# Order of ScalarE's exponentials in a two-state selective scan, and the pace at which two stages are interleaved

## Chip, cores and metric

The kernel runs on one core of one Trainium2 chip. A core has five engines with instruction streams of their own: TensorE (PE in the profile, its weight loads PEld), VectorE (DVE), ScalarE (ACT), GpSimd (POOL) and SyncE (SP), which issues the DMAs. The metric is the device time of one execution in microseconds (us), the median of several runs.

## The reference

Four layers run over an image batch of shape 4 x 64 x 64 x 96. Layers 0 and 1 are selective scans over the image in four directions; layers 2 and 3 are attention without softmax and a quantised feed-forward block. The scan layers take nearly all the time. Each computes, after a group norm, an input projection, a 3x3 depthwise convolution and a SiLU:

```python
xs = jnp.concatenate([xs2, jnp.flip(xs2, axis=-1)], axis=1)        # 4 directions
x_dbl = jnp.einsum('bkdl,kcd->bkcl', xs, x_proj_weight)
dts, Bmat, Cmat = jnp.split(x_dbl, [DT_RANK, DT_RANK + D_STATE], axis=2)
dts = jnp.einsum('bkrl,kdr->bkdl', dts, dt_projs_weight)
delta = jax.nn.softplus(dts + dt_projs_bias[None, :, :, None])
A = -jnp.exp(A_logs).reshape(K, D_INNER, D_STATE)

def step(h, inp):                        # over the 4096 pixels
    u_l, dl, b_l, c_l = inp
    dA = jnp.exp(dl[..., None] * A)
    h = dA * h + (dl * u_l)[..., None] * b_l[:, :, None, :]
    y = jnp.einsum('bkdn,bkn->bkd', h, c_l)
    return (h, y)
```

There are 192 channels and 16 states per channel. The four directions' y are added, normalised over channels, gated with silu(z) and projected back to 96 channels, and the layer's input is added.

## The kernel before, in words

**Units.** A scan layer works on its four images in two pairs, so there are four units (two layers by two pairs). The 2 x 192 channels of a pair fill three tiles of 128 partitions: j = 0 and 1 are 128 channels of one image each ("own"), j = 2 holds 64 channels of each ("shared"). A unit has 48 steps: 4 directions k, 4 chunks ci of T = 1024 pixels, 3 tiles j (`PairScan.steps`).

**Groups.** A step's 16 states are worked two at a time, in eight groups of NG = 2 (`groups` in `PairScan.scan`). For each state the chip needs `exp(delta * A)` and the product `(delta * u) * B`, then one tensor_tensor_scan on VectorE that makes `h`; GpSimd multiplies `h` by C in place, and TensorE adds the states up in PSUM (`yp`) by transposing `h` into it. The letters in `OWN` and `SHARED` (line 45) say which engine makes a state's product:

- V: TensorE selects the row of B into a PSUM tile `bp`, and VectorE multiplies it by `du`.
- A: ScalarE makes the product in transposed form (`x`, `outer`: 8 instructions, 16 for j = 2), and TensorE transposes it into `bp`.
- G: GpSimd multiplies `du` by a row of B that a DMA has spread over the partitions (`dbu`). Then `bp` is free, and ScalarE writes this state's exponential into it.

For V and A the exponential goes into an SBUF tile `da` (four buffers). `bp` has two buffers, one for each state of a group. In letters, a step of an own tile is VA VA VA AG VA VA VA VA, and a step of the shared tile VG VA VA VG VA VG VA VV.

**Order.** Inside the scan all compute engines keep program order (`InOrder`), so the order of the calls in the loop of lines 680 to 730 is the order on each engine. For group g it is:

1. `start_bp` for both states of g (TensorE's products; for a G state ScalarE's exponential into `bp`).
2. `sum_of(g - 3)`: TensorE adds up an older group.
3. `start_ahead(g + 1)`: the next group's `da` and `x` on ScalarE. `start_cb` and `start_dbu` start its DMA and GpSimd's products.
4. VectorE: the V product of g, then its two scans. A group AG has no V product, and its two scans follow each other directly.
5. Pieces of the following steps' preparation (`drive`: `project`, `discretise`), at fixed groups. At state 4 of each step this is softplus (`delta`), followed by `finish_sum`, ScalarE's copy of the finished sum `yp` to `ysum`. Softplus needs another activation table, so there is a table load before it and one before the next exponential.
6. GpSimd: `last` (the carry to the next chunk) and h times C.

**Between the scans.** `between_scans` prepares the next unit (`scan_inputs`: norm, input projection, convolution, first pieces of the scan; a generator with 20 yields) and finishes the unit before (`scan_outputs`: norm over channels, gate, output projection; 16 yields, one for each 256 pixels). Three of these stages are joint: both generators have work, and a loop takes one output and then some inputs in turn. Instructions here do not keep program order strictly; a planner places them at compile time, with the order of the calls as priority. `scan_outputs` takes its tiles from a pool with two buffers, three for the last unit, which runs together with the token layers.

Of the kernel before, what the change touches and what calls it, by code (L numbers as in the profile page):

```python
# [40 lines left out]
NG = 2  # L41
# [100 lines left out]
def between_scans(tc, cst, ident, half, pn, u, before, scan, after):  # L142


    with ExitStack() as stage:
        ins = scan_inputs(tc, stage, cst, ident, half, pn, u, scan, *after)
        if before is not None:
            pp = stage.enter_context(tc.tile_pool(name="c_ps", bufs=2, space=PSUM))
            outs = scan_outputs(tc, stage, cst, ident, half, pn, *before, pp)
            for _ in outs:  # L150
                for _ in range(2):
                    next(ins, None)
        for _ in ins:
            pass
# [117 lines left out]
def scan_outputs(tc, stage, cst, ident, half, pn, layer, pr, pp, turned="pt", summed="po"):  # L272

    nc = tc.nc
    par, zg, x_src, x_dst, y = layer.par, layer.zg[pr], layer.x_src, layer.x_dst, layer.y[pr]
    p2 = stage.enter_context(tc.tile_pool(name="c2", bufs=3 if layer.last and pr else 2))
    if not layer.last:
        norms = [GroupNorm(p2, pn, f"gn{2 * pr + i}", NT // 2) for i in range(2)]
    wo = p2.tile([128, 3, C], F32, name="wo", bufs=1)
# [2 lines left out]
    for g in range(NT // 2):  # L282
# [46 lines left out]
        bufs = 1 if summed == "po" else None  # L329
# [31 lines left out]
def load_weights(nc, pk, w, k):  # L361

    wx = pk.tile([128, 3, NC], F32, name="wx")
    nc.sync.dma_start(out=wx, in_=w["wx"][k])
    wdt = pk.tile([NC, 3, 128], F32, name="wdt")
    nc.sync.dma_start(out=wdt, in_=w["wdt"][k])
    return wx, wdt


class PairScan:  # L370
# [116 lines left out]
    def scan(self, stage, nc):  # L487
        tc, ident, steps, projected, made = self.tc, self.ident, self.steps, self.projected, self.made
# [3 lines left out]
        p2 = stage.enter_context(tc.tile_pool(name="b_2", bufs=2))  # L492
# [4 lines left out]
        def begin_project(k, ci):  # L497
            return self.project(nc, nc.gpsimd, odd if ci % 2 else self.pq, pm, "m1", k, ci)

        def begin_discretise(at):  # L500
            return self.discretise(nc, nc.gpsimd, odd if at % 2 else self.pq, pm, ("m0", "m1"), at)
# [13 lines left out]
        groups = [(at, n) for at in range(len(steps)) for n in range(0, NS, NG)]  # L515
        of = (0, 128, 64)

        def maker(g, i):
            at, n0 = groups[g]
            return (SHARED if steps[at][2] == 2 else OWN)[n0 + i]  # L520

        def exp_of(out, g, i):

            at, n0 = groups[g]
            k, _, j = steps[at]
            col = k * NS + n0 + i
            nc.scalar.activation(out, made[at][0], AF.Exp, scale=amat[:, j // 2, col : col + 1])

        def start_ahead(g):

            at, n0 = groups[g]
            das, xs = {}, {}
            for i in range(NG):
                if maker(g, i) == "A":
                    xs[i] = outer(g, i)
                if maker(g, i) != "G":
                    das[i] = p2.tile([128, T], F32, name="da", bufs=4)
                    exp_of(das[i], g, i)
            return das, xs

        def outer(g, i):

            at, n0 = groups[g]
            j = steps[at][2]
            dut, bt = made[at][2], projected[at // 3][4]
            x = p2.tile([128, T // 128, 128], F32, name="x")
            for t in range(T // 128):
                for im, cols in ((0, slice(0, D1)), (1, slice(D1, 128))) if j == 2 else ((j, slice(0, 128)),):
                    col = NS * im + n0 + i
                    nc.scalar.mul(x[:, t, cols], dut[:, t, cols], bt[:, t, col : col + 1])  # L550
            return x
# [5 lines left out]
            spread(cb, projected[at // 3][2], steps[at][2], n0)  # L557
            return cb

        bbs = {}  # L560

        def start_bb(g):

            at, n0 = groups[g]
            for i in range(NG):
                if maker(g, i) == "G":
                    bbs[g, i] = p2.tile([128, 1, T], F32, name="bb", bufs=1)
                    spread(bbs[g, i], projected[at // 3][2], steps[at][2], 2 * NS + n0 + i)
# [9 lines left out]
        def start_bp(g, i, xs):  # L578


            at, n0 = groups[g]
            _, _, j = steps[at]
            bp = pm.tile([128, T], F32, name="bp", bufs=2)
            if maker(g, i) == "G":
                exp_of(bp, g, i)
            elif maker(g, i) == "A":
                for t in range(T // 128):
                    nc.tensor.transpose(bp[:, 128 * t : 128 * t + 128], xs[i][:, t], ident)
            else:
                for hf in range(2):  # L590
                    cols = slice(512 * hf, 512 * hf + 512)
                    nc.tensor.matmul(
                        bp[:, cols],
                        sel[:, n0 + i, of[j] : of[j] + 128],
                        projected[at // 3][1][:, cols],
                        start=True,
                        stop=True,
                    )
            return bp
# [31 lines left out]
        def start_skip(at):  # L631

            k, _, j = steps[at]
            if k == 0:
                skips[at] = p2.tile([128, T], F32, name="skip", bufs=1)
                nc.scalar.mul(
                    skips[at].rearrange("p (a b) -> p a b", b=HW), projected[at // 3][0][j], dsum[:, j // 2]
                )
# [15 lines left out]
        def load_kept(at):  # L654

            if steps[at][0]:
                kept[at] = p2.tile([128, T // 128, 128], F32, name="kept", bufs=1)
                for tile_, there in places(at, kept[at]):
                    nc.sync.dma_start(out=tile_, in_=there)
# [12 lines left out]
        def sum_of(g):  # L672
            for i in range(NG):
                add_up(g, i, hs[g])
            del hs[g]

        def begun(pieces):
            return [next(pieces), pieces]

        for g, (at, n0) in enumerate(groups):  # L680
            k, ci, j = steps[at]
            rev, first, final = k >= 2, ci == 0, ci == L // T - 1
            if n0 == 0:
                if first and j == 0:
                    last = [pk.tile([128, NS], F32, name=f"last{i}", tag=f"last{i}") for i in range(3)]
                    if k + 1 < K:
                        weights[k + 1] = load_weights(nc, pk, w, k + 1)
                if j == 0:
                    projecting = begun(begin_project(*steps[at + 3][:2])) if at + 3 < len(steps) else []
                discretising = begun(begin_discretise(at + 1)) if at + 1 < len(steps) else []  # L690
            if n0 == 8 and at + 1 < len(steps):
                load_kept(at + 1)
            (da, xs), cb, dbu = ahead, cb_next, dbu_next
            if g + 2 < len(groups):
                start_bb(g + 2)

            bps = [start_bp(g, i, xs) for i in range(NG)]
            if g >= LAG:
                sum_of(g - LAG)
            if n0 == 0:  # L700
                start_skip(at)
            if n0 == NS - NG:
                drive(discretising, n0)
                drive(projecting, (j, n0))
            if g + 1 < len(groups):
                ahead, cb_next, dbu_next = start_ahead(g + 1), start_cb(g + 1), start_dbu(g + 1)

            hs[g] = h = p2.tile([128, NG, T], F32, name="h", bufs=LAG + 1)
            du = made[at][1]
            for i in range(NG):  # L710
                if maker(g, i) == "V":
                    nc.vector.tensor_tensor(bps[i], du, bps[i], ALU.mult)
            way = slice(None, None, -1) if rev else slice(None)
            for i in range(NG):
                nc.vector.tensor_tensor_scan(
                    h[:, i, way],
                    (da[i] if i in da else bps[i])[:, way],
                    (bps[i] if i in da else dbu[i])[:, way],
                    0.0 if first else last[j][:, n0 + i : n0 + i + 1],
                    ALU.mult,  # L720
                    ALU.add,
                )
            drive(discretising, n0)
            if n0 == NG * (LAG - 1) and at > 0:
                finish_sum(at - 1)
            drive(projecting, (j, n0))
            if not final:
                nc.gpsimd.tensor_copy(last[j][:, n0 : n0 + NG], h[:, :, 0] if rev else h[:, :, T - 1])
            for i in range(NG):
                nc.gpsimd.tensor_tensor(h[:, i], h[:, i], cb[:, i], ALU.mult)  # L730
# [363 lines left out]
```

## Time and profile before

The median of three runs is 10643.59 us (10634.33 to 10654.25). The profiled execution took 10644.94 us, its span is 10643.2 us, and all times below are of it.

| | PE | DVE | ACT | POOL |
|---|---|---|---|---|
| busy us in the span | 8055.8 | 9608.1 | 8760.2 | 9008.7 |
| share | 76% | 90% | 82% | 85% |
| busy in 5200 to 7500 (a scan stage) | 1753.31 | 2173.41 | 1988.56 | 2153.91 |
| busy in 7500 to 7720 (a joint stage) | 179.58 | 136.35 | 123.86 | 28.13 |

From first to last, the span holds a first preparation (to about 156 us), scan 0, a joint stage from about 2461 to 2680, scan 1, a joint stage to about 5199, scan 2, a joint stage to about 7715, scan 3 to about 10014, and the token layers with the last outputs.

A row of groups gives line, engine, operation, the tiles written and read, shapes and number, then busy time and mean length of one, then the idle time of the engine ahead of them and what ended it. Nearly all scan instructions carry line 71, that of the helper that keeps their order, so they are told apart by their tiles. Durations of one instruction that matter: a scan 2.3 us, a V product 1.2 us, an exponential 1.1 us, the eight x together 2.4 us (sixteen 3.9 us), GpSimd's h times C 2.36 us.

### The profile page before, as it was taken

How to read it: one execution, taken by the hardware profiler on the slowest of the kernel's cores; microseconds unless marked ns; L12 is line 12 of the kernel's file. 1: busy time of each engine (PE TensorE's matmuls, PEld its weight loads, DVE VectorE, ACT ScalarE, POOL GpSimd, SP SyncE). 2: the span in 40 equal slices, each digit the busy share in tenths (PEclk: the TensorE clock that was granted, in tenths of full speed). 3: DMA queues.
4: the chain of work that ended last, by engine and by line, in shares of the span. 5: the costliest groups of instructions: out<-in, count | busy, mean ns of one | idle time of the engine just before them, and what ended most of it. 6: DMA issues, size and time to landing. Idle time of an engine off the chain costs nothing. (4 is left out here: it accounts for less than half of the span.)

```text
span 10643.2 us, 142480 instructions
## 1 busy us (share of the span) xinstructions
PE 8055.8 (76%) x47648; PEld 5971.9 (56%) x47648; DVE 9608.1 (90%) x6922; ACT 8760.2 (82%) x18779; POOL 9008.7 (85%) x5298
## 2 busy tenths in 40 slices
PE   7777777777777777777877777777777777777666
PEld 4555555554555555555455555555455555555554
DVE  8999999997899999998899999999699999999755
ACT  6888888885888888887688888888598888888666
POOL 3999999993899999997499999999299999999745
PEclk9888899988888898988888988998888889899877
DMA  4677777775667777777467777777566777777710
GB/s 154 208 211 215 216 222 218 219 213 158 196 210 216 217 220 220 219 214 210 149 209 211 220 219 218 220 219 217 143 209 211 213 220 219 220 217 219 199 35 25
DMA packets 905175, 2120.41 MB, mean 199 GB/s; under 512 B 330583, under 2 KB 640153, under 8 KB 706713
## 3 DMA queue, kind: packets, MB, share of 16 engines
q1 hardware_dynamic: 904440, 2111.30, 68.3%
q8 instruction: 378, 6.19, 0.2%
q14 instruction: 357, 2.92, 0.1%
HBM read 1949.56 MB, written 161.48 MB: 198 GB/s over the span
## 5 line engine op out<-in xcount | busy, mean ns | idle before, releaser
L71 POOL TENSOR_TENSOR h<-h,cb 128x1024 f32<-128x1024 f32 x3072 | 7191.2, 2364 | 234.4 <-issue 58.6
L71 DVE TENSOR_TENSOR_SCAN h<-da,last,bp 128x1024 f32<-128x1024 f32 x2064 | 4736.8, 2335 | 147.1 <-PE bp L71 23.8
L71 ACT ACTIVATE x<-dut,bt 128x128 f32<-128x128 f32 x12288 | 3494.8, 370 | 1.5 <-PE bp L71 1.1
L71 PE MATMUL yp<-ident,h 128*128 128x128 f32 x24576 | 3370.2, 297 | 9.8 <-POOL h L71 9.8
L71 PEld LDWEIGHTS yp<-ident,h 128*128 128x128 f32 x24576 | 3197.1, 157 | 125.7 <-issue 75.5
L71 ACT ACTIVATE da<-delta,amat 128x1024 f32<-128x1024 f32 x2752 | 3060.2, 1138 | 96.0 <-DVE h L71 94.9
L71 PE MATMUL bp<-ident,x 128*128 128x128 f32 x10240 | 1679.2, 316 | 1282.1 <-DVE h L71 923.7
L71 PEld LDWEIGHTS bp<-ident,x 128*128 128x128 f32 x10240 | 1362.6, 162 | 1840.7 <-ACT x L71 1026.7
L71 DVE TENSOR_TENSOR bp<-du,bp 128x1024 f32<-128x1024 f32 x1472 | 1780.1, 1213 | 266.0 <-PE bp L71 264.4
L71 DVE TENSOR_TENSOR_SCAN h<-da,bp 128x1024 f32<-128x1024 f32 x688 | 1537.7, 2274 | 52.7 <-ACT da L71 11.4
L71 PE MATMUL bp<-bparts,sel 96*128 96x512 bf16 x2944 | 918.8, 398 | 760.4 <-DVE h L71 741.2
L71 PEld LDWEIGHTS <-sel 96*128 96x128 bf16 x2944 | 226.8, 100 | 1554.8 <-DVE h L71 1043.7
L71 ACT ACTIVATE bp<-delta,amat 128x1024 f32<-128x1024 f32 x320 | 358.1, 1119 | 528.3 <-DVE h L71 526.3
L71 POOL TENSOR_TENSOR dbu<-du,bb 128x1024 f32<-128x1024 f32 x320 | 754.6, 2358 | 0.0
L71 DVE TENSOR_TENSOR_SCAN h<-bp,last,dbu 128x1024 f32<-128x1024 f32 x240 | 558.9, 2329 | 10.4 <-POOL dbu L71 7.1
L81 POOL TENSOR_TENSOR ln_rs<-ln_ve,half 128x4 f32<-128x4 f32 x64 | 82.4, 1288 | 567.2 <-DVE ln_ve L79 442.0
L71 PE MATMUL xps<-u,wx 128*76 128x512 f32 x720 | 532.0, 824 | 0.0
L71 ACT ACT_TABLE_LOAD x380 | 487.5, 1283 | 34.6 <-DVE gn_norm L138 22.4
L71 POOL COPY last<-h 128x2 f32<-128x2 f32 x1152 | 215.8, 187 | 351.0 <-DVE h L71 349.1
L71 POOL TENSOR_TENSOR du<-delta,u 128x1024 f32<-128x1024 f32 x188 | 496.2, 2639 | 0.0
L71 ACT COPY ysum<-yp 128x1024 f32<-128x1024 f32 x192 | 194.4, 1012 | 300.3 <-PE yp L71 300.3
L71 PE MATMUL dps<-cdt,wdt 12*128 12x512 f32 x752 | 435.0, 658 | 0.0
(159 smaller groups left out, 6328.0 us busy)
## 6 DMA issues: line engine op xcount, KB each, us to landing
cb<-crow SPq DMA_DIRECT2D x1024, 1024.0 KB
cb<-crow SPq DMA_DIRECT2D x1024, 512.0 KB
bb<-crow SPq DMA_DIRECT2D x384, 256.0 KB
bb<-crow SPq DMA_DIRECT2D x128, 512.0 KB
y<-ysum SPq DMA_DIRECT2D x192, 256.0 KB
kept<-y SPq DMA_DIRECT2D x160, 256.0 KB
y<-ysum SPq DMA_DIRECT2D x64, 512.0 KB
zt<-zg SPq DMA_DIRECT2D x64, 384.0 KB
```

The source lines that it names most:

```text
L71: return self.tc.keep_in_program_order(getattr(self.engine, op)(*args, **kwargs))
L81: nc.gpsimd.tensor_tensor(rs, ve, half, ALU.pow)
```

## The change

There are three edits.

- In the scan, ScalarE's exponential of a G state is no longer issued in `start_bp`. It is put on a list `late`, and `start_ahead(g + 1)` issues it after the next group's `da` exponentials. In the same function all `da` now come first and the products `x` last. For the unit's last group the list is emptied directly.
- In the joint stages an output is followed by one input, and each fourth output by two, in place of two inputs after each output.
- `scan_outputs` takes its tiles from a pool with three buffers for every unit.

```diff
@@ between_scans
-            for _ in outs:
-                for _ in range(2):
+            for g, _ in enumerate(outs):
+                for _ in range(2 if g % 4 == 3 else 1):
                     next(ins, None)
@@ scan_outputs
-    p2 = stage.enter_context(tc.tile_pool(name="c2", bufs=3 if layer.last and pr else 2))
+    p2 = stage.enter_context(tc.tile_pool(name="c2", bufs=3))
@@ PairScan.scan
             for i in range(NG):
-                if maker(g, i) == "A":
-                    xs[i] = outer(g, i)
                 if maker(g, i) != "G":
                     das[i] = p2.tile([128, T], F32, name="da", bufs=4)
                     exp_of(das[i], g, i)
+            while late:
+                exp_of(*late.pop(0))
+            for i in range(NG):
+                if maker(g, i) == "A":
+                    xs[i] = outer(g, i)
             return das, xs
@@
-        bbs = {}
+        bbs, late = {}, []
@@ start_bp
             if maker(g, i) == "G":
-                exp_of(bp, g, i)
+                late.append((bp, g, i))
@@ the loop over groups
-            if g + 1 < len(groups):
+            if g + 1 == len(groups):
+                while late:
+                    exp_of(*late.pop(0))
+            else:
                 ahead, cb_next, dbu_next = start_ahead(g + 1), start_cb(g + 1), start_dbu(g + 1)
```

## The prediction

> **What bounds the kernel now.** I read the page first, then busy times by stage.
>
> ```profile
> span 10643.2 us, 142480 instructions
> PE 8055.8 (76%) x47648; PEld 5971.9 (56%) x47648; DVE 9608.1 (90%) x6922; ACT 8760.2 (82%) x18779; POOL 9008.7 (85%) x5298
> ...
> L71 ACT ACTIVATE bp<-delta,amat 128x1024 f32<-128x1024 f32 x320 | 358.1, 1119 | 528.3 <-DVE h L71 526.3
> ```
>
> ```profile
> 2700.00:5000.00 2300.00, 1736.95 (x10624) 1321.41 (x10623) 2160.28 (x1155) 1971.99 (x4236) 2150.53 (x1214) 0.89 0.74 215
> ```
>
> The third line is the exponential that the change moves: 320 of them, 358 us of work, and 528 us in which ScalarE stood idle ahead of them until VectorE freed the PSUM buffer. The other fence is one of four scan stages (columns: length, then busy PE, PE weight load, DVE, ACT, POOL). In 2300 us DVE is busy 2160, POOL 2151, ACT 1972. ACT has 328 us of slack per stage, so its idle time is worth something only if DVE waits for it. The table of waits in 2800 to 4900 us says whether it does (in total, times, longest):
>
> ```profile
> ACT bp L71 <- DVE h L71: 113.3, 48, 5.5
> ...
> DVE bp L71 <- PE bp L71: 61.8, 77, 1.7
> DVE h L71 <- ACT x L71: 1.7, 1, 1.7
> DVE h L71 <- ACT da L71: 0.5, 1, 0.5
> ```
>
> DVE waits 61.8 us for PE's products into bp and some 2 us for ACT. So the scan's bound is DVE, then PE's in-order chain behind DVE's releases; ACT's 113 us wait is off the path. What matters is how early each ACT result is. This is the timeline at a group "AG" (state 6 built by ScalarE, state 7 by GpSimd), start and length in us:
>
> ```profile
> 3402.40 1.15 ACT L71 ACTIVATE da<-delta,amat 128x1024 f32<-128x1024 f32 x1 [0.92 <-DVE h L71]
> 3409.19 1.15 ACT L71 ACTIVATE da<-delta,amat 128x1024 f32<-128x1024 f32 x1
> 3411.65 1.27 ACT L71 ACTIVATE delta<-dps,par 128x512 f32<-128x512 f32 x2
> 3414.39 1.01 ACT L71 COPY ysum<-yp 128x1024 f32<-128x1024 f32 x1 [1.47 <-PE yp L71]
> 3415.42 1.28 ACT L71 ACT_TABLE_LOAD   x1
> 3417.27 1.12 ACT L71 ACTIVATE bp<-delta,amat 128x1024 f32<-128x1024 f32 x1 [0.57 <-DVE h L71]
> 3421.70 2.18 ACT L71 ACTIVATE da<-delta,amat 128x1024 f32<-128x1024 f32 x2
> ```
>
> ```profile
> 3412.65 6.82 DVE L71 TENSOR_TENSOR_SCAN h<-da,last,bp 128x1024 f32<-128x1024 f32 x3
> 3419.39 2.32 DVE L71 TENSOR_TENSOR_SCAN h<-bp,last,dbu 128x1024 f32<-128x1024 f32 x1
> ```
>
> The third scan of the last-but-one line is AG's first (3417.16); AG has no VectorE product, so its GpSimd scan follows 2.24 us later. Its exponential ends at 3418.39, one microsecond in time. ACT came to it at 3416.70, after softplus, ysum and a table load. Two exponentials in a row take 2.18 us, so they are 1.05 apart.
>
> The joint stages, in 20 us pieces (same columns):
>
> ```profile
> 2520.00:2540.00 20.00, 16.61 (x46) 7.38 (x45) 20.00 (x31) 16.57 (x32) 1.00 (x1) 1.00 0.72 214
> 2600.00:2620.00 20.00, 18.50 (x63) 9.22 (x62) 14.65 (x35) 10.81 (x19) 2.89 (x2) 1.00 0.34 99
> 2640.00:2660.00 20.00, 14.00 (x42) 8.49 (x41) 10.89 (x37) 8.42 (x20) 2.01 (x2) 0.61 0.53 158
> ```
>
> DVE and PE are near full until about 2611 and 2631, then half busy: all inputs are done and the last six outputs run alone at some 7 us each, PE at a clock of 0.6.
>
> [...] no ACT instruction passes the waiting exponential. [...] here eight transposes take 1.06 us in most groups and 1.94 in those behind long PE gaps. [...]
>
> **Part 1, the order on ScalarE.** Nothing is added or removed: 2752 da, 320 bp, 12288 x stay, and no DMA or wait moves. Three results move.
>
> *da of a group's second state* goes ahead of x, 2.4 us earlier. It may wait: with four da buffers it needs the second scan two groups back. Behind it on ACT is x. With ACT as far ahead as buffers allow, before: da, x, da from the first scan's end; after: da, da (2.3 us later), x. At 3402.40 that gives da 3402.40, da 3404.7, x 3405.74 to 3408.1. Its transposes start at 3411.54, so x is still 3 us early. Worth nothing either way; the cover is that margin.
>
> *x of the group after a GpSimd state.* At 3349.67 (same timeline, earlier) the exponential waited 4.66 us, and now two da (2.1 us) fill that wait. But x then ends 0.2 us after its group begins, and PE starts the transposes at 0.23 either way (DVE frees bp then). Gain: nothing on DVE.
>
> *The exponential itself* goes behind two da: 2 x 1.05 = 2.10 us later, where ACT did not arrive early. Who waits for it is the GpSimd scan. By kind of group:
> - 64 "VG" at SHARED's start: ACT arrives 4.7 us early: nothing. 64 at states 10 and 11: 2.6 early: nothing.
> - 64 VG at states 6 and 7: ACT arrives 0.6 us after the group's start (mean), the scan comes at 3.6. Unmoved, the end would be at 0.6 + 2.1 + 1.2 = 3.9; ACT is also some 2 us earlier there, from the filled wait. Between nothing and 0.5 x 64 = 33 us; I take 10.
> - 128 AG (two in each three-step cycle): the scan comes 2.24 us after the start. The exponential ends at arrival + 2.10 + 1.12[...]: stall = arrival + 1.04.
>
> Arrival at AG, from the trace (end of the instruction before each exponential, against AG's first scan): 73 of 128 at -0.3 to -1.0, 51 at 0.8 to 1.4 (ysum waits long for PE: 4.02 us at 320.30), 4 at unit starts at 3.2. In the first class the work ahead also moves. Follow the order from 3404.7: x to 3408.1; da at 3409.19 (its buffer comes then); AG's x 3410.24 to 3412.6; table load to 3413.9; softplus to 3415.1; ysum, ready since 3414.3, to 3416.1; table load to 3417.4. Arrival is +0.24 instead of -0.46. So 73 x (0.24 + 1.04) = 93; 51 x (1.05 + 1.04) = 107, where PE's wait hides the shift; 4 x 2.1 = 8. Together **+208 us**. The floor, if arrival did not slip (-0.45), is 0.6 x 124 = 75.
>
> Late next: DVE's stall delays everything behind it one for one, since no DVE wait is on POOL (3 us behind at AG, it only catches up). PE's idle time ahead of the next transposes grows from about 1.7 to 3 us; if the clock drops, transposes and sums end some 2 us later and the product two groups on, 0.6 to 0.9 us in hand, comes late: 0 to 0.7 x 128 = 90; I take **+40**.
>
> **Part 2, the joint stages.** `ins` has 20 yields, `outs` 16. Before, two inputs per output: inputs end with the tenth. After, 1, 1, 1, 2: both end together. No work changes. A stage runs from its first DVE work, 2472.7, to the scan's first, 2679.7: 207 us with 156.6 busy on DVE (sum of the pieces); PE has about 160 without the slow-clock tail. At the 91 to 93% that DVE and PE reach while both parts run, 157 to 160 us need about 172: from 2477 to 2649, plus 5 for the norms: 25 us less. The new end has its own tail (a nine-tap chain of 11 us, the scan's beginnings), so I take 20 x 3 = **-60**; between nothing and -35 x 3 = -105.
>
> **Part 3, three buffers.** Loads of ys (9.5 us of DVE waits in the stage), zt and xr start one output sooner; SP stands less long with stores and xn loads queued behind. This makes the 10 us pace per output possible and is counted in part 2. The last pair had three already.
>
> **Sum.** 208 + 40 + 10 - 60 = +198, on a profiled run of 10644.9 us (span 10643.2; median of the runs 10643.6): **10842 us**.
>
> **Rivals.**
> - *Faster.* ACT, rid of 528 us of standing still, arrives at AG more than 1.05 us before it starts; no stall, and the joint stages decide: 10644 - 60 = 10584. For it: the filled waits. Against: at AG only 0.36 to 0.40 us (mean) was stood still, and arrival is set by PE's sum, ysum and a table load. It decides where arrival is below -1.04. Chance 0.13.
> - *Break-even.* Arrival stays at its floor, PE stays warm, joint gain full: 75 - 75 = 0, 10644. Chance 0.10.
> - *PE cold and joint stages no better* (PE is as full as DVE; order alone gives nothing): 208 + 90 + 33 - 10 = +321, 10965. Chance 0.17.
> - My case: 0.60, own range 10760 to 10920.
>
> 0.2% (21 us) is about what a measurement of this kernel can tell from no change. Faster 0.13; same 0.05 and slower 0.05 from the break-even case; slower in all 0.82. The range leaves out the faster case and the far end of the third: 10670 to 10940.
>
> **What would show it.** VectorE's GpSimd scans (h from bp, last, dbu) wait for "ACT bp" some 1.3 us or more in most AG groups (9 us in total before), and hardly in VG; ACT's wait ahead of bp falls from 528 to under 100 us; scan stages grow by about 60 us each; joint stages shrink from 207 to about 187. I am wrong if AG's scans start on time, if x is what PE waits for, or if the joint stages give over 35 us each.

## The result and the profile after

The changed kernel takes 10923.81 us (median; 10918.27 to 10934.13) against 10643.59 (10644.94 when a fourth run of the kernel before is counted in). The ratio is 1.0264, 95% interval 1.025 to 1.0278: it is slower by some 280 us. The forecast was slower by 198 us, 10842, with a range up to 10940. The sign and the main mechanism were right, and the size was short by 82 us. The time lies inside the stated range, and 4 us above the 10920 at which the prediction's own case ended.

The profiled execution after took 10934.13 us. These are the lines of its page that answer to those shown of before, with three rows beside them (a row: busy us, mean ns of one, then the engine's idle time ahead of them and what ended it):

```profile
span 10932.0 us, 141669 instructions
...
PE 8270.5 (76%) x47648; PEld 6251.2 (57%) x47648; DVE 9635.9 (88%) x6922; ACT 8842.4 (81%) x18779; POOL 9031.9 (83%) x5298
...
L71 ACT ACTIVATE da<-delta,amat 128x1024 f32<-128x1024 f32 x2752 | 3083.2, 1144 | 753.7 <-DVE h L71 739.0
...
L71 DVE TENSOR_TENSOR bp<-du,bp 128x1024 f32<-128x1024 f32 x1472 | 1783.3, 1215 | 406.0 <-PE bp L71 403.8
...
L71 DVE TENSOR_TENSOR_SCAN h<-bp,last,dbu 128x1024 f32<-128x1024 f32 x240 | 560.7, 2336 | 162.8 <-ACT bp L71 152.1
...
L71 ACT ACTIVATE bp<-delta,amat 128x1024 f32<-128x1024 f32 x320 | 354.1, 1107 | 133.8 <-DVE h L71 133.8
```

ScalarE's idle time ahead of the moved exponentials fell from 528.3 to 133.8 us, as the change means it to (the forecast said under 100). But more than that came back ahead of `da`: 753.7 us there, where it was 96.0. And VectorE's GpSimd scans, which hardly waited for ScalarE before, now do.

The stages, after (columns: length, then busy PE, PE weight load, DVE, ACT, POOL, clock, DMA share, GB/s; the first line is a piece of the second scan stage, the second lies in a joint stage):

```profile
2745.00:5130.00 2385.00, 1815.22 (x10643) 1410.99 (x10644) 2177.35 (x1150) 2006.94 (x4269) 2153.68 (x1197) 0.86 0.73 207
5136.00:5330.00 194.00, 164.53 (x506) 82.79 (x506) 152.56 (x315) 112.27 (x221) 32.71 (x37) 0.91 0.53 150
```

VectorE does the work of a scan stage in nearly the same busy time, but spread over more of it: 91% where it was 94%. Adding up from the trace, with a scan stage taken from its first VectorE work to the end of its last scan:

| us | before | after | difference | forecast |
|---|---|---|---|---|
| four scan stages | 9192.8 | 9536.3 | +343.5 | +258 |
| three joint stages | 222.8, 219.2, 219.6 | 207.8, 202.1, 201.4 | -50.3 | -60 |
| first preparation and token layers | 788.7 | 784.4 | -4.3 | 0 |

The sum is +288.8, the difference of the two spans. In the scan stages, VectorE's idle time by what ended it:

| VectorE waits in scans, us | before | after | difference | forecast |
|---|---|---|---|---|
| for ACT bp (the late exponentials) | 9.1 | 214.4 | +205 | +208 +10 |
| for PE bp (products) | 290.6 | 447.6 | +157 | +40 |
| for POOL dbu | 21.4 | 5.4 | -16 | 0 |

VectorE's table of waits in 2700 to 5000 us, after (in total, times, longest), has both at the top:

```profile
DVE bp L71 <- PE bp L71: 99.5, 115, 1.9
DVE h L71 <- ACT bp L71: 53.7, 30, 3.2
```

So the first term of the forecast holds to 3 us. The waits for PE grew by 157 us where 40 was forecast; not all of this is the wait that the forecast meant, and the last sections take it apart. One group shows both waits. ScalarE at a group AG that starts on VectorE at 3508.35, after the change (start, length):

```profile
3505.19 1.26 ACT L71 ACTIVATE delta<-dps,par 128x512 f32<-128x512 f32 x2
3506.35 1.01 ACT L71 COPY ysum<-yp 128x1024 f32<-128x1024 f32 x1
3507.38 1.28 ACT L71 ACT_TABLE_LOAD   x1
3508.67 2.19 ACT L71 ACTIVATE da<-delta,amat 128x1024 f32<-128x1024 f32 x2
3510.77 1.10 ACT L71 ACTIVATE bp<-delta,amat 128x1024 f32<-128x1024 f32 x1
```

VectorE at the same group:

```profile
3503.85 6.83 DVE L71 TENSOR_TENSOR_SCAN h<-da,last,bp 128x1024 f32<-128x1024 f32 x3
3511.97 2.35 DVE L71 TENSOR_TENSOR_SCAN h<-bp,last,dbu 128x1024 f32<-128x1024 f32 x1 [1.29 <-ACT bp L71]
...
3521.12 1.23 DVE L71 TENSOR_TENSOR bp<-du,bp 128x1024 f32<-128x1024 f32 x1 [1.06 <-PE bp L71]
```

The table load ends at 3508.66, 0.3 us after AG's start (the forecast worked out 0.24 for this case). Two `da` go first, the exponential ends at 3511.87, and AG's second scan starts 1.29 us late (forecast 1.28). Two groups on, at 3521.12, VectorE waits again, 1.06 us, this time for PE. Here is PE in between:

```profile
3514.46 1.48 PE L71 MATMUL bp<-ident,x 128*128 128x128 f32 x8 [2.88 <-DVE h L71]
3515.74 3.21 PE L71 MATMUL yp<-ident,h 128*128 128x128 f32 x16
...
3520.47 0.61 PE L71 MATMUL bp<-bparts,sel 96*128 96x512 bf16 x2
```

PE stood idle for 2.88 us ahead of the eight transposes, since VectorE freed `bp` late. The transposes then take 1.48 us and the sixteen of the sum 3.21 us; where the granted clock over them is 0.95 of full speed or more they take 1.06 and 1.91 (medians of this trace, 753 and 1045 cases). That is 1.7 us more in all, and the product two groups behind AG (3520.47) ends just before VectorE's late start at 3521.12. The trace also keeps the clock that PE was granted: over these 1.48 us it is 0.67 of full speed.

### The profile page after: what moved, and what is told of

Same layout as the page of the kernel before. It is cut to its first block, busy times and chain, and to the rows that moved or that the text cites. A ratio compares the mean times of both kernels' runs of the same rounds, so it can differ in the third digit from the quotient of the medians.

```text
span 10932.0 us, 141669 instructions
## 1 busy us (share of the span) xinstructions
PE 8270.5 (76%) x47648; PEld 6251.2 (57%) x47648; DVE 9635.9 (88%) x6922; ACT 8842.4 (81%) x18779; POOL 9031.9 (83%) x5298
## 5 line engine op out<-in xcount | busy, mean ns | idle before, releaser
L71 ACT ACTIVATE da<-delta,amat 128x1024 f32<-128x1024 f32 x2752 | 3083.2, 1144 | 753.7 <-DVE h L71 739.0
L71 PE MATMUL yp<-ident,h 128*128 128x128 f32 x24576 | 3570.0, 308 | 10.2 <-POOL h L71 10.2
L71 PEld LDWEIGHTS yp<-ident,h 128*128 128x128 f32 x24576 | 3395.7, 164 | 130.3 <-issue 80.4
L71 PE MATMUL bp<-ident,x 128*128 128x128 f32 x10240 | 1754.5, 328 | 1397.3 <-DVE h L71 1199.3
L71 PEld LDWEIGHTS bp<-ident,x 128*128 128x128 f32 x10240 | 1441.7, 169 | 1894.9 <-ACT x L71 1015.4
L71 DVE TENSOR_TENSOR bp<-du,bp 128x1024 f32<-128x1024 f32 x1472 | 1783.3, 1215 | 406.0 <-PE bp L71 403.8
L71 DVE TENSOR_TENSOR_SCAN h<-da,bp 128x1024 f32<-128x1024 f32 x688 | 1538.0, 2275 | 50.9 <-PE bp L71 12.0
L71 ACT COPY dut<-dups 128x512 f32<-128x512 f32 x376 | 215.7, 574 | 340.0 <-PE dups L71 340.0
L71 ACT ACTIVATE bp<-delta,amat 128x1024 f32<-128x1024 f32 x320 | 354.1, 1107 | 133.8 <-DVE h L71 133.8
```

Source lines behind the costliest of these rows:

```text
L71: return self.tc.keep_in_program_order(getattr(self.engine, op)(*args, **kwargs))
```

## Experiments

All runs below are timed against the kernel before, and the ratios are medians with their 95% interval. VectorE's waits are sums over the profiled execution.

| kernel | median us | ratio to before | waits ACT bp | waits PE bp |
|---|---|---|---|---|
| after | 10923.81 | 1.0264 [1.025, 1.0278] | 214.4 | 447.6 |
| joint stages only | 10600.01 | 0.9961 [0.9947, 0.9976] | 9.6 | 296.8 |
| scan only | 10977.64 | 1.0319 [1.0301, 1.0336] | 211.6 | 436.4 |
| after, AG's exponential where it was | 10627.67 | 0.9983 [0.9974, 0.9991] | 4.7 | 361.9 |
| joint stages, and the order of da and x | 10644.1 | 1.0005 [0.9996, 1.0013] | 6.2 | 356.5 |
| after, late exponential behind one da | 10710.4 | 1.0067 [1.0052, 1.0082] | 78.9 | 369.8 |
| after, PE kept busy behind AG | 10773.47 | 1.0129 [1.0113, 1.0144] | 204.6 | 321.1 |

**The two halves apart.** First the joint stages alone (the pace of outputs and inputs, and the third buffer), then the scan's part alone.

```diff
 before + joint stages only
-            for _ in outs:
-                for _ in range(2):
+            for g, _ in enumerate(outs):
+                for _ in range(2 if g % 4 == 3 else 1):
...
-    p2 = ...tile_pool(name="c2", bufs=3 if layer.last and pr else 2))
+    p2 = ...tile_pool(name="c2", bufs=3))
```

> The kernel before with the new pace of the joint stages and the third buffer; the scan is untouched. My theory (the joint stages gained 15 to 18 us each in the changed kernel's trace, 50 us in all, and the scan lost about 343): 10595 us, scan stages at 2295 to 2301 us as before, ScalarE's wait ahead of the bp exponentials back at some 528 us. Rival (the joint stages only look shorter in the changed kernel because the scan begins later on ScalarE): 10640 us, no change.

> The kernel before with the new order on ScalarE alone. My theory: the whole loss is here, 10644 + 343 = 10985 us, each scan stage 78 to 92 us longer; VectorE waits some 214 us for ACT's bp and some 448 us for PE's bp. Rival (the two parts disturb each other, for instance through the SP queue at the start of a scan): clearly under 10960.

The joint stages alone give 10600.01, the scan alone 10977.64: -44 and +334 against 10643.59. The two sum to +290 and were measured together at +280, so they hardly touch each other. The joint stages shrink to 204.5, 201.4 and 201.1 us. The loss is the scan's alone.

**AG's exponential back in its place.** All else stays as changed; only where the group's first state is ScalarE's, the exponential is issued in `start_bp` again.

```diff
 after + AG's exponential first
             if maker(g, i) == "G":
-                late.append((bp, g, i))
+                if maker(g, 0) == "A":
+                    exp_of(bp, g, i)
+                else:
+                    late.append((bp, g, i))
```

> The changed kernel, but in groups AG the GpSimd state's exponential is issued where it was before; in groups VG it still goes behind the next group's two exponentials, and x still comes last. My theory (the loss is the AG scan's wait and what it sets off on PE): 10595 us, like the joint stages alone; VectorE waits under 15 us for ACT's bp and about 290 us for PE's bp. Rival (x behind both da, issued later in all groups, makes PE late): the extra 157 us of waits for PE stay, about 10750 us.

It takes 10627.67: putting AG's exponential back takes off 296 us, more than the whole 280. The rows of VectorE of this kernel:

```profile
L71 DVE TENSOR_TENSOR bp<-du,bp 128x1024 f32<-128x1024 f32 x1472 | 1781.4, 1214 | 344.1 <-PE bp L71 342.1
...
L71 DVE TENSOR_TENSOR_SCAN h<-bp,last,dbu 128x1024 f32<-128x1024 f32 x240 | 559.1, 2330 | 7.7 <-POOL dbu L71 5.2
```

The waits for the late exponential are gone (214.4 to 4.7), and with them 86 us of the waits for PE (447.6 to 361.9): 210 + 86 = 296. The run missed its expectation by 33 us on the slow side, because the waits for PE did not fall back to 290. Something in the scan's part other than AG's exponential makes PE late.

**Only the order of da and x.** To the joint stages alone one thing is added: in `start_ahead` both `da` come first and `x` last, while every exponential of a G state stays in `start_bp`.

```diff
 joint stages only + order of da and x
             for i in range(NG):
-                if maker(g, i) == "A":
-                    xs[i] = outer(g, i)
                 if maker(g, i) != "G":
                     ...
                     exp_of(das[i], g, i)
+            for i in range(NG):
+                if maker(g, i) == "A":
+                    xs[i] = outer(g, i)
```

> The new joint stages, and in the scan only the order of da and x: both exponentials of the next group first, x last; the GpSimd states' exponential stays where it was before. My theory, after the run with AG's exponential first (10628 us[...]): x behind AG ends about 1.05 us later than before, some 1.6 us after its group begins, PE's gap ahead of it grows and the clock drops, 10625 us with 340 to 360 us of waits for PE. Rival (as in the prediction, the order of da and x is free): 10600 us and 297 us.

The order costs 44 us: 10644.1 against 10600.01, where 25 was expected and the prediction had nothing. The trace shows two places. The first is behind AG. PE's waits for `x` over the whole execution, with the joint stages alone:

```profile
PE bp L71 <- ACT x L71: 318.6, 216, 3.1
```

and with the order of da and x on top:

```profile
PE bp L71 <- ACT x L71: 418.2, 273, 4.1
```

In the group behind AG, the last `x` now ends 1.4 to 1.7 us after the first transpose has begun (mean; before, 0.3), so that PE takes the transposes at ScalarE's pace. The expectation named a dropped clock as the cause, and it isn't: the clock granted over these transposes is 1.00 and 0.99 (first and second tile, mean), as good as with the joint stages alone (1.00 and 0.98). VectorE's idle time ahead of the product two groups behind AG grows by 37 us (3.4 to 40.6). The second place is the group of a tile's states 14 and 15. ScalarE there, with the order of da and x:

```profile
3425.46 1.15 ACT L71 ACTIVATE da<-delta,amat 128x1024 f32<-128x1024 f32 x1 [0.38 <-DVE h L71]
3426.52 2.43 ACT L71 ACTIVATE x<-dut,bt 128x128 f32<-128x128 f32 x8
3428.85 0.57 ACT L71 COPY dut<-dups 128x512 f32<-128x512 f32 x1
```

and PE of the same kernel:

```profile
3429.47 0.66 PE L71 MATMUL dups<-ident,du 128*128 128x128 f32 x4 [1.09 <-ACT dut L71]
...
3431.66 1.03 PE L71 MATMUL bp<-bparts,sel 96*128 96x512 bf16 x2
```

The second `da` waits for a buffer. `x` stands behind it, and behind `x` stands `dut`, the copy that frees PE's PSUM tile `dups` for the next step's `du`. PE waits for that copy (1.09 us here, and 139.3 us in the whole execution, where it was 89.1 before), and the next V product is queued behind PE's transposes of `du`. VectorE's idle time ahead of states 14 and 15 of the own tiles grows by 36 us (50.4 to 86.6).

With this run the whole difference falls into steps, each between two kernels that differ in one edit: joint stages -44, the order +44, the late exponentials of the VG groups -16 (10644.1 to 10627.67; the two ratios' intervals don't overlap, and by the ratios it is 23), AG's late exponential +296. The sum is +280. The gain that moving the exponentials can bring exists, but it is some 20 us. What a step is worth depends on the edits already made: AG's late exponential was tried only with the new order of da and x.

**Behind one `da` instead of two.** The forecast's stall was arrival + 1.04: 2.10 for two `da` and 1.12 for the exponential less 2.24, and the rest was the author's allowance for the step from the exponential to the scan. Measured, that step is 0.10 us (median of the 127 scans that waited for their exponential in the trace after). Issuing the late exponential between the two takes 1.05 us off the term for the two.

```diff
 after + exponential behind one da
                     exp_of(das[i], g, i)
-            while late:
-                exp_of(*late.pop(0))
+                while late:
+                    exp_of(*late.pop(0))
             for i in range(NG):
```

> The changed kernel, but the late exponential is issued behind the next group's first exponential in place of its second: 1.05 us earlier. My theory (stall = arrival + 1.04 us per AG group): every AG stall shrinks by 1.05 us, from 1.3 and 2.05 to 0.25 and 1.0, so the waits for ACT's bp fall from 214 to about 80 us, and the waits for PE from 448 to about 350: 10924 - 134 - 98 = 10690 us. Rival (the stall has a threshold, such as a missed order on PE, and is not graded): no change from 10924, or all of the loss gone, 10595.

It takes 10710.4, and VectorE's waits for the late exponential are 78.9 us where 80 was expected. The stall is what the position in ScalarE's queue makes it, `da` by `da`.

**PE kept busy behind AG.** To see whether the slow transposes are the clock, eight matmuls are put ahead of the transposes of the group behind AG, into the gap in which PE waits. Nothing reads what they write; all of the kernel's work is done beside them.

```diff
 after + eight matmuls ahead of the x transposes of the group behind AG
             elif maker(g, i) == "A":
+                if g and maker(g - 1, 1) == "G" and maker(g - 1, 0) == "A":
+                    spare = pm.tile([128, 512], F32, name="spare", tag="m0")
+                    for _ in range(8):
+                        nc.tensor.matmul(spare, sel[:, n0 + i, of[j] : of[j] + 128],
+                            projected[at // 3][1][:, :512], start=True, stop=True)
```

> The changed kernel with eight idle matmuls (96x512 bf16, into a PSUM bank that nothing reads in that group) on PE behind the V product of each group that follows AG, ahead of its transposes: they fill the gap in which PE stands still while VectorE waits. My theory (the extra waits for PE come from PE's half clock after a gap of 3 us): transposes there take 1.06 us in nearly all groups, not 1.94 in six of ten, the waits for PE's bp fall from 448 to about 330 us, 10924 - 118 = 10806 us. Rival (not the clock but PE's order behind a later start): 10924 or more.

More work on PE makes the kernel 150 us faster, 10773.47, while the waits for ScalarE stay (214.4 to 204.6). PE at the same group as shown above, of this kernel:

```profile
3514.14 1.06 PE L71 MATMUL bp<-ident,x 128*128 128x128 f32 x8 [1.16 <-DVE h L71]
...
3518.48 0.61 PE L71 MATMUL bp<-bparts,sel 96*128 96x512 bf16 x2
```

The transposes are back at 1.06 us, and the product follows their start by 4.34 us instead of 6.01. `x` was ready in both kernels (it ends 0.2 us ahead of the first transpose, mean), so what changed is the clock, and the granted clock in the traces says the same: over the transposes of the group behind AG its mean is 0.99 and 0.98 before (first and second tile), 0.61 and 0.70 after, and 0.98 in both tiles with the matmuls. Counting eight transposes as slow where they start more than 0.16 us apart (0.11 is the usual step), that group is slow in 0 and 2% of cases before, in 61 and 56% after, and in 2 and 3% with the matmuls. PE's idle time in the 4 us ahead of the transposes is 1.6 us before, 3.0 after and 1.3 with the matmuls. The kernel with the exponential behind one `da` lies between: 2.0 us of idle, a granted clock of 0.82 and 0.87. So in the groups behind AG, 3.0 us of idle out of 4 went with slow transposes in six cases of ten. Other places of the kernel before show a lower clock behind idle time as well: at states 0 and 1 of the first tile it is 3.2 us of idle and a clock of 0.50, at states 4 and 5 of the second 1.2 us and 0.77 (means of 64 steps each), so these means give no limit of the idle time. The clock records of the traces before and after hold two values alone, 1.0 and 0.5 of full speed (392 stretches of each before, 526 after), and each stretch between the first and the last change lasts a multiple of 3.41 us (1 to 45 of them before, 1 to 31 after). In both, the eight transposes take 1.06 us where the clock over them is 0.95 or more, and 1.94 where it is under 0.55 (medians).

**The local wait at states 14 and 15.** On top of the last kernel, `x` goes ahead of the second `da` in that one group.

```diff
 PE kept busy behind AG + x first at states 14 and 15
             for i in range(NG):
+                if maker(g, i) == "A" and n0 == NS - NG:
+                    xs[i] = outer(g, i)
...
-                if maker(g, i) == "A":
+                if maker(g, i) == "A" and n0 != NS - NG:
                     xs[i] = outer(g, i)
```

> The run with PE kept warm, and one thing more: in the last group of each own step (states 14 and 15) x goes ahead of the second da again, as before the change. Behind them on ScalarE stands the copy dut, and PE's next transposes (dups) and products wait for that copy. My theory (the second da waits for VectorE, x and dut wait behind it, and PE stands 1.09 us for dut in place of 0.33): VectorE's waits for PE's bp fall from 321 to about 285 us, the waits at that group from 0.66 to 0.3 us, and the time from 10773 to 10738 us. Rival (the wait at that group comes from elsewhere, such as a shift of the whole group): 10773 us, no change.

This missed: 10769.38, ratio 1.0122 [1.0105, 1.0139], no better than without it. The wait itself went away. PE's transposes of `du` in this kernel:

```profile
L71 PE MATMUL dups<-ident,du 128*128 128x128 f32 x1504 | 237.9, 282 | 0.3 <-ACT dut L71 0.3
```

Their idle time is 0.3 us where it is 139.2 after the change, and VectorE's idle time at these groups falls from 0.64 us (first tile) and 0.62 (second) to nothing (means). But other gaps grew by as much: at the AG group of the first tile from 2.08 to 2.70 us, and in the shared tile from 0.92 to 1.24 (states 4 and 5) and from 0.72 to 1.00 (states 14 and 15). Why the AG group's stall grows there is open.

**What in the joint stages gives the gain.** The pace alone, and the third buffer alone, each on the kernel before; the edits are the two halves of the first diff above.

> The kernel before with the new pace of the joint stages, two buffers. My theory (the pace alone shortens the tail, a third buffer lets the outputs keep it): 10615 us, about 30 of the 50 us. Rival (outputs cannot keep the pace with two buffers): 10644 or slower.

> The kernel before with three buffers in the outputs' pool, old pace. My theory: the last six outputs of a joint stage, which run alone at some 7 us each, overlap a little more: 10630 us. Rival (they are bound by PE at a slow clock and by their own chain): 10644, no change.

The pace alone gives 10600.17 (0.9964 [0.9951, 0.9978]), the buffer alone 10601.01 (0.9964 [0.9952, 0.9977]), both together 10600.01. Each gives all of it, more than the 10615 and 10630 that were expected. VectorE's last additions of a joint stage, two neighbours of before:

```profile
2666.18 0.68 DVE L337 TENSOR_TENSOR xo<-xr,po 96x512 f32<-96x512 f32 x1 [3.67 <-PE po L335]
...
2673.02 0.68 DVE L337 TENSOR_TENSOR xo<-xr,po 96x512 f32<-96x512 f32 x1 [3.74 <-PE po L335]
```

and two neighbours with the third buffer alone:

```profile
2631.29 0.68 DVE L337 TENSOR_TENSOR xo<-xr,po 96x512 f32<-96x512 f32 x1 [0.33 <-PE po L335]
...
2634.03 0.68 DVE L337 TENSOR_TENSOR xo<-xr,po 96x512 f32<-96x512 f32 x1
```

Before, the outputs that run alone at the end come some 7 us apart (4.5 to 9.2 in this stage), and nearly all wait for PE. With a third buffer the first four of them overlap and come 2.7 to 4.2 us apart; the last two keep their 7. With the new pace there is no such end: the outputs are spread over the stage. Either cure leaves nothing for the other.

**What the moved exponential is worth once PE isn't late.** PE's chain is the second bound, so it is shortened first: the sum of an older group goes between the two products of a group rather than behind both. Once on the joint stages alone, once on the changed kernel.

```diff
 joint stages only, and after: sum between the products
-            bps = [start_bp(g, i, xs) for i in range(NG)]
+            bps = [start_bp(g, 0, xs)]
             if g >= LAG:
                 sum_of(g - LAG)
+            bps.append(start_bp(g, 1, xs))
```

> The joint stages' part alone, and in the scan PE adds up the group three back (sum_of) between the products of the group's first and second state, no longer behind both. PE then works in the gap in which it waits for VectorE to free the second bp, and its chain behind that release is shorter by 1.9 us. My theory (VectorE's remaining waits are for that chain): the waits for PE's bp fall from 290 to under 100 us, 10595 - 190 = 10405 us; GpSimd, busy 2151 of 2300 us in a scan stage, may take back up to 60. Rival (the sums come too early for GpSimd's products and hold up the transposes behind them): slower than 10595.

> The changed kernel with PE's sums between the products of a group's two states. My theory (the waits for ACT's bp behind AG are set on ScalarE and do not depend on PE's order; the extra waits for PE are PE's chain at half clock, which now has work in the gap): waits for ACT's bp stay at 190 to 220 us, waits for PE's bp fall from 448 to about 250 us, 10924 - 190 = 10735 us. Rival (ScalarE comes late to AG because PE's sum is late, so an earlier sum mends the stall too): waits for ACT's bp under 130 us and 10650 us or less.

Without the scan's change this takes 10541.2 (0.9909 [0.9894, 0.9923]): 59 us better than the joint stages alone, far from the expected 195. The waits for PE fell only to 245.1 us, since a new one of 1.2 us (mean) arose in the shared tile, in the group behind the VG at states 6 and 7. PE waits there for `ysum` (1.66 us in one such group). The supposition is that ScalarE comes late to `ysum` for having stood ahead of the exponential at the step's start; the last run tests it. With the change it takes 10651.04 (1.0011 [1.0004, 1.0018]), 84 us better than expected and close to the rival's time. PE's waits fall to 197 us, and so does part of AG's stall (ACT bp 214.4 to 175.2), as ScalarE's `ysum` waits 64 us for PE's sum instead of 187.

If that holds, the new wait in the shared tile is of the kind that the change is meant for. So, on the sum between the products, only the VG groups' exponentials are made late, and `x` goes last only where one is held. All other groups keep the old order.

```diff
 sum between the products + VG's exponential late
             das, xs = {}, {}
+            held = bool(late)
             for i in range(NG):
-                if maker(g, i) == "A":
+                if maker(g, i) == "A" and not held:
                     xs[i] = outer(g, i)
                 ...
+            while late:
+                exp_of(*late.pop(0))
+            for i in range(NG):
+                if maker(g, i) == "A" and held:
+                    xs[i] = outer(g, i)
...
             if maker(g, i) == "G":
-                exp_of(bp, g, i)
+                if maker(g, 0) == "A":
+                    exp_of(bp, g, i)
+                else:
+                    late.append((bp, g, i))
```

> The kernel with PE's sums between the two products, and of the change's order on ScalarE only what concerns groups VG: their exponential goes behind the next group's two, with that group's x last; all other groups keep the order of before. In the run without it VectorE waited 1.15 us for PE at the group behind the second VG of the shared step, PE for ysum, and ScalarE had stood 5.3 us ahead of the first VG's exponential. My theory (with PE's chain shortened ScalarE is the late one in shared steps, and the filled wait is now worth something): that wait goes, 64 x 1.1 = 70 us, 10470 us. Rival (ScalarE's wait is still off the path): 10541 us, no change, or slower through x.

It takes 10413.27, ratio 0.9789 [0.9773, 0.9805], which beats both kernels. Of its page:

```profile
span 10410.7 us, 142318 instructions
...
PE 7934.8 (76%) x47648; PEld 5887.7 (57%) x47648; DVE 9592.6 (92%) x6922; ACT 8771.7 (84%) x18779; POOL 9013.7 (87%) x5298
...
L71 DVE TENSOR_TENSOR bp<-du,bp 128x1024 f32<-128x1024 f32 x1472 | 1775.9, 1210 | 79.2 <-PE bp L71 76.6
```

VectorE's products wait 79.2 us, where they waited 406.0 with the change. The late exponentials of the VG groups, worth 16 us in the changed kernel, are worth 128 here (10541.2 to 10413.27; the later `x` behind a VG group is in this figure, while the 16 us were measured with `x` last everywhere). The wait in the group behind the VG at states 6 and 7 is gone, as supposed (1.16 us to 0.00, mean). What comes next is in sight too: VectorE's waits for GpSimd's `dbu`, 21.4 us before, are 69.1.

## Why the forecast was right in sign and short in size

Read by place from the two profiled executions, VectorE's idle time in the scans grew by 212 us ahead of AG's second scan, by 104 us ahead of the product two groups behind AG (4.6 to 108.7), by 32 us ahead of states 14 and 15 of the own tiles (50.9 to 82.7) and by 11 us ahead of AG's first scan. At VG groups it fell by 12.

- **AG's scans wait for the late exponential, +208: right.** Measured +205 for all G scans. ScalarE's work ahead ends 0.31 us (forecast 0.24) and 1.09 us (1.05) after the group's start, as worked out. How many groups fall in each class was not: 62 and 63, where the forecast took 73 and 51. The first class waits 82 us where 93 was forecast and the second 130 where it was 107, so part of the close sum is luck. Putting the exponential back, and moving it by one `da`, changed the waits as the formula says.
- **"If the clock drops ... 0 to 0.7 x 128 = 90; I take +40": mis-sized.** The mechanism is as told: PE's idle time in the 4 us ahead of the transposes grew (1.6 to 3.0 us), the clock over them dropped (0.99 and 0.98 to 0.61 and 0.70), they slowed (0 and 2% of cases to 61 and 56%), and the product two groups on was late. The term is the 104 us at that product, of which 2.3 us are left with the matmuls. The middle of the bounds was a choice with no evidence, and the upper bound was too low as well: VectorE waits 1.12 us (first tile) and 0.58 us (second) there, mean, against at most 0.7. (The reason given for the delay, that no VectorE wait is on GpSimd, was not quite so: 21.4 us were.)
- **"da of the second state goes ahead of x ... worth nothing either way": the step that failed.** Alone it is +44 us. The cover named was `x`'s own margin of 3 us, read at AG. It was not looked up at the group behind AG, where `x` moved behind one more `da` and, in the kernel with the order alone, ended over 1 us too late. Nor was the queue followed past `x`: `dut` stands there, PE's `du` transposes wait for `dut`, and the next product stands behind those. In the changed kernel this second place remains: the 32 us ahead of states 14 and 15.
- **"x of the group after a GpSimd state ... gain: nothing on DVE": right only as the change stands.** There, VectorE's stall delays the transposes until `x` is done. With the order alone, `x` is what PE waits for, which the forecast named as a way to be wrong.
- **Second VG, +10: nothing was seen.** No VG scan waits for ScalarE in the trace after; the VG groups' late exponentials bring 16 us.
- **Joint stages, -60: somewhat high.** They gave -50 in the profile and -44 in the medians. Which part of the estimate was too large is not shown.
- **"This makes the 10 us pace per output possible", of the third buffer: wrong.** The pace gives its whole gain with two buffers, and the buffer gives the same gain at the old pace.

By the medians' steps the sum should have read 296 + 44 - 16 - 44 = +280, where the forecast had 208 + 40 + 10 - 60 = +198. The 82 us are 48 of AG's exponential, 44 of the order, and 16 of the joint stages, less 26 of VG. But this split depends on the order of the steps: with the order alone 37 us of idle time arise at the product two groups behind AG, where in the changed kernel the clock is the cause. By place, in the profiled executions (+289, so 91 short), it is 64 us of the clock's term, 32 at states 14 and 15, 15 at AG and 10 of the joint stages, less 22 at VG and 8 elsewhere.

The rival "faster" fell at its stated point: ScalarE arrives at AG 0.3 or 1.1 us after the start in nearly all groups, not over 1.04 ahead of it. The rival "PE cold and joint stages no better" (10965) had its first half right and its second wrong; its time was 41 us off, nearer than the forecast.

## What to carry to other kernels

An engine's idle time that no one on the path waits for is not a gain to be had: taking away 394 us of it here moved it to other instructions, and made the one result late that had no slack, that of the group with no product ahead of its scan. When an instruction is moved in a queue that is kept in program order, as those of the scan are here, follow the queue past it to the last instruction that another engine waits for, group kind by group kind; the margin of the moved one alone says nothing of those behind it. And a saving that is small while another chain ends the wait should be tried again once that chain is short: the same late exponential went from some 20 to 128 us.

## What the runs showed of the hardware

Two things were not expected. Eight more matmuls on PE behind every AG group made the kernel faster by 150 us, as they brought the granted clock over the next eight transposes back from 0.61 and 0.70 to 0.98. Behind AG, 3.0 us of idle in the 4 ahead went with slow transposes in 61 and 56% of cases, 1.6 us (the kernel before) in 0 and 2%, and 1.3 us (with the matmuls) in 2 and 3%. And slow transposes alone do not tell the cause: with the order of da and x they passed the same mark (more than 0.16 us a step) while the clock wasn't the reason; `x` was still being written under them, and ended 1.4 to 1.7 us after the first had begun. The end of `x` against the first transpose, and the granted clock over the transposes (1.00 and 0.99 there), tell the two apart.
